# Two graph-attention layers on one core: shorter links between edge pieces, one exponential, a two-piece first product, counts kept, one-hot columns by twos

## The chip, the core and the metric

The kernel runs on 1 core of one Trainium2 chip. A core has a matrix engine (TensorE; PE in the profile, its weight loads PEld), a vector engine (VectorE; DVE), a scalar engine for pointwise functions (ScalarE; ACT), a general engine (GpSimd; POOL), which here issues the gathers, and a sync engine (SyncE; SP), which issues the other transfers. Each engine works through its own instructions in their order; between engines semaphores keep the order. TensorE writes its products to PSUM, which has eight banks.

The metric is the device time of one execution in microseconds: 4405.09 us is the median of 20 runs (4392.43 to 4416.41). The profile page and the trace are of one execution of its own.

## The reference

A graph of 6250 nodes and 200000 edges, sorted by destination, goes through a layer norm with a relu and then through two graph-attention layers, the first with 4 heads of 64, the second with 1 head of 256:

```python
h = jnp.maximum(_layernorm(x, axis=-1), 0.0)
...
te = relu(edge_attr @ We0 + be0) * exp(x @ Wo0 + bo0)[src][:, None]
s2, d2, ea2 = _add_self_loops(src, dst, te, n)
x = relu(_gat(x, s2, d2, ea2, Wg0, as0, ad0, Wge0, ae0, bg0, n, HEADS, PH) + x)
...
def _gat(x, src, dst, ea, Wg, a_s, a_d, Wge, a_e, b, n, h, f):
    hx = (x @ Wg).reshape(n, h, f)
    he = (ea @ Wge).reshape(-1, h, f)
    al = leaky_relu(einsum(hx, a_s)[src] + einsum(hx, a_d)[dst] + einsum(he, a_e), 0.2)
    m = segment_max(al, dst, num_segments=n)
    al = exp(al - m[dst])
    al = al / segment_sum(al, dst, num_segments=n)[dst]
    out = segment_sum(hx[src] * al[:, :, None], dst, num_segments=n)
    return out.reshape(n, h * f) + b
```

A self loop is added to each node, with the mean of its edges' features (their sum divided by their count). So each layer needs, for each destination node, a maximum over its edges, an exponential, and sums of 256 weighted features, of the weights, of the edge features' logits and of the count.

## The kernel before

The 200000 edges are cut into 66 steps (`cuts`): 64 of 24 chunks of 128 edges and two at the end of 14 and 13. Both layers run the same 66 steps, 132 in all, laid out by hand in `edges` (L555 to L653); the last step of a layer is `last` (L655). A prologue computes the node table of layer 0 (`T[0]`: each node's 256 features, its logit parts, its layer-norm numbers).

In a step, 128 partitions hold the step's edges in order, partition p the edges 24p to 24p+23. In the order of the program, for step k (`st`), with nx the step after, pv the one before, pf the one before that:

- SP loads: for every pair of steps the one-hot row numbers `lb` of the pair that comes next (`load_lb`, when k is even; 384 KB), the table rows `tw` of nx's nodes (`nodes`, L834) and in layer 0 their input rows (L836), the edge features `ea` of a pair (`load_ea`, 768 KB, one buffer), the flags `fl` (`load_fl`, every second step, one buffer), and the index tables of a group of four steps. At the step's end SP stores the row of the next layer's table (`rows3`, L1203).
- POOL: 24 gathers (L775) of one table row for each of 128 edges, into one of three buffers `G`. A buffer is free when the sums of the step three before are done.
- `rphase1(nx)`: the first product of the edge features (L853) in four pieces, each into one of two PSUM buffers of one bank (`y`), evicted with a relu by ScalarE (L854).
- `logits(st)`: VectorE adds the parts of the attention logits and runs two scans (L951, L953), a forward and a backward running maximum within each partition.
- `ends(st)`: two TensorE transposes of the scans' ends (L964, L965), which ScalarE brings to SBUF as `LF` (L967).
- `spread(nx)`: VectorE turns nx's row numbers into one-hot columns in place (L870, 128x768) and makes the selection matrix `Q` (L872). Then `parts(nx)` (L892 to L895) splits the destination logits of `tw` into three bf16 parts, and TensorE multiplies them with Q (L897).
- `sums(pv)`: 24 products of one-hot matrices and `G` (L1068), accumulated in one bank.
- `links(st)`: over the 128 partitions, one scan each way (L984, L985) joins the maxima of destinations that run over several partitions, with the flags of which partitions belong together added (L981), and starts from the step before (L979); two small transposes (L990) bring them back. They stand behind `sums(pv)` on TensorE.
- `blocks(nx)`, `onehots(st)` (L882: 24 one-hot matrices by one comparison), `finish(pf)`: the merging of the sums with the self loop (`merge`, then `nodes0` or `nodes1`). `merge` computes from the count column a reciprocal and a mark for nodes without edges (L1091 to L1094).
- `evict(pv)`, `carry(pv)`, `rows1(pf)`: ScalarE and TensorE work on the sums; `rphase2(nx)`, `adst(nx)`: further products for nx's logits.
- `maxima(st)`: VectorE takes the maximum of both scans and both links (L1000 to L1010, the first link waits for L990), subtracts it (L1012), ScalarE computes the exponential twice, once into PSUM for the scaling (L1014) and once into `G` for the sums (L1015); for the edges that continue from the step before there is a third small one (L1025 to L1029).
- `scale(st)`: `G` times the weights, in pieces of 12 chunks (L1058). `carried(st)`: the carried sum is added to the first edge's row. `edge_rows(nx)`: the logits of nx's edges are turned (L925) for the next step.

Between the layers `added` (L739) adds to the first step's gathered rows, chunk by chunk, the rows of the last 256 nodes, which were not in the table yet when they were gathered: for each of 24 chunks two products into a `y` buffer (L745) and an addition by VectorE (L748).

Of the kernel before, what the change touches and what calls it, by code (L numbers as in the profile page):

```python
# [22 lines left out]
F32 = mybir.dt.float32  # L23
BF = mybir.dt.bfloat16
# [7 lines left out]
P = 128  # L32
# [46 lines left out]
class Kernel:  # L79
# [27 lines left out]
    def consts(self, wp):  # L107
# [45 lines left out]
        self.k_iota, self.k_part, self.k_w = k[:, 0:P], k[:, P:P + 1], k[:, 2 * P:2 * P + 4 * C]  # L153
# [205 lines left out]
    def fixed_rows(self):  # L359
        nc, cp = self.nc, self.cp  # L360
        self.crow = cp.tile([1, D + self.L[0].H], F32, name="crow")
        self.cl = [cp.tile([4, 2, P], F32, name=f"cl{i}") for i in range(2)]
        for t in self.cl:
            nc.gpsimd.memset(t[:, 1, P - 1:P], -BIG)
# [20 lines left out]
    def indices(self, wp):  # L385
# [11 lines left out]
        r4 = wp.tile([NS, 4, P], I32, name="r4", bufs=1)  # L397
        nc.sync.dma_start(r4, a["prow"])
        nc.sync.dma_start(self.src, a["src"])
        yield  # L400
        scf = wp.tile([P, 11, NS], F32, name="scf", bufs=1)
# [28 lines left out]
        fl = wp.tile([NS, 3, P], F32, name="fl", bufs=1)  # L430
        wh = wp.tile([NS, 2, P], F32, name="wh", bufs=1)
        V.tensor_tensor(fl[:, 0, :], r4[:, 0, :], r4[:, 3, :], op=OP.is_equal)
        V.tensor_tensor(wh[:, 0, :], r4[:, 2, :], r4[:, 3, :], op=OP.is_equal)
        yield
        V.tensor_tensor(wh[:, 1, :], r4[:, 0, :], r4[:, 1, :], op=OP.is_equal)
        V.tensor_tensor(fl[:, 1:3, :], wh, fl[:, 0:1, :].to_broadcast([NS, 2, P]), op=OP.mult)
        yield
        V.tensor_scalar(fl, fl, 1.0, BIG, op0=OP.subtract, op1=OP.mult)
        self.flags = self.dp.tile([NS, 3, P], F32, name="flags")
        nc.sync.dma_start(self.flags, fl)  # L440
# [61 lines left out]
    def index_group(self, g, pool, di):  # L502
# [22 lines left out]
        for pen, e in ((self.fpen, 0), (self.lpen, c - 1)):  # L525
            t = pool.tile([P, 4 * C], F32, name="gt", bufs=2)
            ends = d3[:, :, e:e + 1].to_broadcast([P, n, c])
            V.tensor_sub(v3(t[:, :w]), *((ends, d3) if e else (d3, ends)))
            yield
            V.tensor_scalar(pen[:, o:o + w], t[:, :w], 1.0, -BIG, op0=OP.min, op1=OP.mult)  # L530
            yield
# [23 lines left out]
    def edges(self, ctx):  # L555
# [7 lines left out]
        self.ps_y = self.pool("ps_y", 2, ctx, space=PSUM)  # L563
        self.ps_1 = self.pool("ps_1", 1, ctx, space=PSUM)
        self.ps_f = self.pool("ps_f", 1, ctx, space=PSUM)
        offs = np.concatenate([[0], np.cumsum(self.cs)]).tolist()
# [144 lines left out]
    def redirect(self):  # L711
# [6 lines left out]
        lt = self.wp.tile([P, 4 * C], F32, name="mt")[:, :c]  # L718
# [20 lines left out]
    def added(self, st, rows):  # L739

        nc, L, c = self.nc, st["L"], st["C"]
        for i in range(self.early):
            ps = self.ps_y.tile([P, 512], F32, name="y")
# [42 lines left out]
    def load(self, k, name, tile, part):  # L786
# [3 lines left out]
        for i, st in enumerate(q):  # L790
            st[name] = tile[:, i]
# [25 lines left out]
    def load_fl(self, k):  # L817
        if self.pair(k):
            H = self.steps[k]["L"].H
            self.load(k, "fl", self.lp.tile([4, 2, 3, P], F32, name="fl", bufs=1), lambda s, e, st: (  # L820
                lambda t: t[:H], self.flags[s:e].partition_broadcast(H)))
# [22 lines left out]
    def rphase1(self, st):  # L844
        nc, L = self.nc, st["L"]
        l, ea = L.l, st["ea"]
        st["R"] = R = self.wp.tile([P, 2, 32 * C], F32, name="R", bufs=1)
        for i in range(2):
            r = slice(i * PH, (i + 1) * PH)
            for w, _ in self.halves(st):  # L850
                n = w.stop - w.start
                y = self.ps_y.tile([P, 512], F32, name="y")
                nc.tensor.matmul(y[:, :n], self.webd[l][r, :], ea[r, w], start=True, stop=True)  # L853
                nc.scalar.activation(R[:, i, w], y[:, :n], AF.Relu, bias=self.be[l])  # L854
                yield
# [9 lines left out]
    def spread(self, st):  # L865


        lb, n = st["lb"], 32 * st["C"]
        V = self.nc.vector
        V.tensor_tensor(lb[:, :n], lb[:, :n], self.k_part.to_broadcast([P, n]), op=OP.is_equal)  # L870
        st["Q"] = Q = self.wp.tile([P, P], BF, name="Q")
        V.tensor_tensor(Q.rearrange("p (k j) -> p k j", j=32), self.k_iota[:, 0:32].unsqueeze(1).to_broadcast([P, 4, 32]),  # L872
# [555 lines left out]
```

## Time and profile before

| | |
|---|---|
| median of 20 runs | 4405.09 us (4392.43 to 4416.41) |
| the profiled execution | 4419.34 us, of which its span 4417.6 us |
| PE busy | 2853.4 us (65%), granted clock 0.768 |
| VectorE busy | 2932.0 us (66%), 7162 instructions |
| ScalarE busy | 688.0 us (16%) |
| POOL busy | 2977.4 us (67%), of which 3114 gathers 2960.9 |
| moved by DMA | 584.83 MB, 132 GB/s over the span |

The span is the time from the first to the last instruction that the profile shows. A group or a timeline row names the line, the engine, the operation, what it writes and reads, the shapes, and in brackets how long its engine had been idle before it and what ended that idling. "issue" is idle time in which the engine waited for nothing that the profile shows. Layer 0 takes the first half of the span (to about 2385 us), layer 1 the second.

### The profile page before, as it was taken

The numbers are of one execution on the slowest core, as the hardware profiler recorded it, in microseconds if no ns is written. First come the engines' busy times: TensorE is split into PE (matmuls) and PEld (weight loads), VectorE is DVE, ScalarE is ACT, GpSimd is POOL, SyncE is SP. The second block draws the span as 40 slices with busy tenths as digits, with TensorE's granted clock in tenths as the row PEclk, the third lists the DMA queues.
The fourth block names the chain that finished last, engine by engine and source line by source line (L and its number), as shares of the span: only waits on it lengthen the run. The fifth ranks groups of instructions, "written<-read, shape, count | busy, mean of one in ns | idle before, by whom it ended". The sixth has DMA issues, their size and how long they took to land. (4 is left out here: it accounts for less than half of the span.)

```text
span 4417.6 us, 37687 instructions
## 1 busy us (share of the span) xinstructions
PE 2853.4 (65%) x10408; PEld 1869.3 (42%) x10408; DVE 2932.0 (66%) x7162; ACT 688.0 (16%) x1910; POOL 2977.4 (67%) x3155
## 2 busy tenths in 40 slices
PE   6756666666666666666665766666666666666665
PEld 5434333343434334343433544434434434434434
DVE  7766676676767667666776666666666666666665
ACT  5111111111111111111111111111111111111110
POOL 2766666666666666666663777777777777777774
PEclk9777777777777777777777878778778778778777
DMA  7554444545444454544442455555555555455552
GB/s 221 144 131 120 128 129 128 132 119 134 118 131 129 129 134 115 134 117 128 126 132 82 133 141 143 142 140 136 135 142 143 142 139 136 135 141 143 142 134 68
DMA packets 246387, 584.83 MB, mean 132 GB/s; under 512 B 62904, under 2 KB 103310, under 8 KB 246104
## 3 DMA queue, kind: packets, MB, share of 16 engines
q0 software_dynamic: 150144, 422.82, 37.4%
q1 hardware_dynamic: 95610, 158.89, 11.6%
q8 instruction: 83, 1.36, 0.1%
q14 instruction: 134, 1.10, 0.1%
q10 hardware_dynamic: 416, 0.67, 0.0%
HBM read 547.87 MB, written 34.37 MB: 132 GB/s over the span
## 5 line engine op out<-in xcount | busy, mean ns | idle before, releaser
L775 POOL DMA_INDIRECT G<-T,src x3114 | 2960.9, 951 | 1382.7 <-issue 902.5
L1068 PE MATMUL u<-G,S 128*128 128x270 f32 (+1 forms) x6252 | 1735.1, 445 | 7.0 <-issue 4.9
L1068 PEld LDWEIGHTS u<-G,S 128*128 128x128 f32 x6252 | 1384.0, 224 | 310.4 <-issue 5.5
L1058 DVE TENSOR_TENSOR G<-G,kps 128x3072 f32<-128x3072 f32 (+1 forms) x270 | 862.9, 3238 | 61.9 <-ACT kps L1014 61.7
L853 PE MATMUL y<-ea,webd 64*128 64x384 f32 (+1 forms) x1056 | 500.3, 604 | 381.2 <-ACT R L854 375.1
L853 PEld LDWEIGHTS y<-ea,webd 64*128 64x128 f32 x1056 | 210.1, 222 | 600.1 <-ACT R L854 481.2
L882 DVE TENSOR_TENSOR S<-kps,loc 128x3072 f32<-128x3072 f32 (+2 forms) x133 | 434.7, 3268 | 0.2 <-ACT kps L1014 0.2
L964 PE MATMUL lf<-ident,bw 128*4 128x128 f32 (+1 forms) x132 | 48.8, 370 | 594.6 <-DVE bw L953 594.6
L854 ACT ACTIVATE R<-y,webd 128x384 f32<-128x384 f32 (+2 forms) x528 | 295.4, 572 | 373.7 <-PE y L853 358.1
L897 PE MATMUL zad<-a,Q 128*128 128x12 bf16 (+1 forms) x132 | 24.9, 189 | 461.1 <-DVE LF L979 427.1
L964 PEld LDWEIGHTS lf<-ident,bw 128*4 128x4 f32 (+1 forms) x132 | 10.7, 81 | 706.0 <-DVE bw L953 685.6
L1004 DVE SCALAR_TENSOR_TENSOR m<-fpen,lf,m 128x24 f32<-128x24 bf16 (+1 forms) x66 | 16.6, 251 | 350.1 <-PE lf L990 350.1
L892 DVE CAST a<-tw 128x4 bf16<-128x4 f32 (+1 forms) x132 | 22.6, 171 | 319.1 <-DMA tw<-T 319.0
L897 PEld LDWEIGHTS <-Q 128*128 128x128 bf16 x132 | 13.7, 104 | 512.3 <-DVE LF L979 490.7
L862 PE MATMUL zad<-R,wea 128*64 128x384 f32 (+1 forms) x1056 | 201.6, 504 | 0.3 <-DVE aq L904 0.3
L939 DVE TENSOR_TENSOR G<-rt,G 128x96 f32<-128x96 f32 (+1 forms) x132 | 30.2, 229 | 247.3 <-DMA G<-T,src 242.2
L1007 DVE TENSOR_TENSOR mt<-fpen,lf 128x96 f32<-128x96 bf16 (+1 forms) x66 | 16.6, 252 | 262.6 <-PE lf L990 262.6
L1073 ACT ACTIVATE U<-u 128x270 f32<-128x270 f32 (+1 forms) x132 | 51.8, 393 | 773.0 <-PE u L1068 773.0
L967 ACT ACTIVATE LF<-lf 4x256 f32<-4x256 f32 (+1 forms) x132 | 49.4, 374 | 595.4 <-PE lf L965 595.3
L925 DVE STREAM_TRANSPOSE rt<-zad 128x768 f32<-128x768 f32 (+1 forms) x130 | 124.4, 957 | 11.5 <-PE zad L911 11.5
L870 DVE TENSOR_TENSOR lb<-lb,kps 128x768 bf16<-128x768 bf16 x132 | 121.1, 918 | 12.1 <-DMA lb<-locrow 12.1
L1117 ACT ACTIVATE mw<-mw 128x8 f32<-128x8 f32 x66 | 13.8, 208 | 717.7 <-DVE mw L1116 717.7
(206 smaller groups left out, 2641.4 us busy)
## 6 DMA issues: line engine op xcount, KB each, us to landing
G<-T,src POOLq DMA_INDIRECT x3114, 2.8
ea<-in_ea_dram SPq DMA_DIRECT2D x64, 768.0 KB
lb<-locrow SPq DMA_DIRECT2D x64, 384.0 KB
T<-t1row SPq DMA_DIRECT2D x66, 260.0 KB
tw<-T SPq DMA_DIRECT2D x66, 258.0 KB
tw<-T SPq DMA_DIRECT2D x66, 134.0 KB
tw<-in_x_dram SPq DMA_DIRECT2D x66, 128.0 KB
out_dram<-fb SPq DMA_DIRECT2D x64, 128.0 KB
```

Of the source, the lines that this page charges most:

```text
L775: nc.gpsimd.indirect_dma_start(out=G[:, c, 0:L.TW], out_offset=None, in_=self.rows[L.l][0:n * (1 + L.l), :], in_offset=bass.IndirectOffset ...
L853: nc.tensor.matmul(y[:, :n], self.webd[l][r, :], ea[r, w], start=True, stop=True)
L854: nc.scalar.activation(R[:, i, w], y[:, :n], AF.Relu, bias=self.be[l])
L862: nc.tensor.matmul(st["zad"][i * PH:(i + 1) * PH, o], self.wea[l][0], R[:, i, w], start=True, stop=False)
L870: V.tensor_tensor(lb[:, :n], lb[:, :n], self.k_part.to_broadcast([P, n]), op=OP.is_equal)
L882: nc.vector.tensor_tensor(st["S"][:, c0:c1, :], self.k_iota.unsqueeze(1).to_broadcast(w), self.loc[:, o + c0:o + c1].unsqueeze(2).to_broad ...
L925: V.transpose(rv[:, :32 * c].rearrange("p (b n) -> p b n", b=2), z.rearrange("p (b n) -> p b n", b=2)[:, :, :16 * c])
L964: nc.tensor.transpose(pl[0:H, P + 1:2 * P + 1], bv[:, :, 0], self.ident)
L967: nc.scalar.activation(lf[:H, 1:2 * P + 1], pl[0:H, 1:2 * P + 1], AF.Copy)
L1058: nc.vector.tensor_tensor(v, v, pw[:, c0:c1, :].unsqueeze(3) .to_broadcast([P, c1 - c0, H, L.F]), op=OP.mult)
L1068: nc.tensor.matmul(u[:, :L.W], S[:, i, :], G[:, i, 0:L.W], start=(j == 0), stop=(j == c - 1))
L1073: self.nc.scalar.activation(U[:, :L.W], st["u"][:, :L.W], AF.Copy)
```

## The change

Line numbers of the kernel after are higher by up to 31. What it does, part by part:

- *Links and ends.* Forward and backward scans now write one tile `fb`, so that the ends of both lie at one stride, those of the backward scan 32 columns on. One transpose of 36 columns (`ends`) brings them to partitions 0 to 3 and 32 to 35 of a PSUM tile `lf` that is kept for the whole run, with its first column at -1e38. The link scans read it there, with no eviction, with no addition of a first flag and with no column from the step before: both flags and the penalties at each piece's first and last edge (`fpen`, `lpen`) now compare with the neighbouring edge across the border. The result is one tile of 36 rows, turned back by one transpose.
- *One exponential.* The carried part's argument is put behind the weights' arguments in the constant tile `mt`, one activation covers all, and VectorE copies the weights to `G`.
- *Scaling* takes 24 chunks in one instruction.
- *First product.* `y` is one buffer of two banks; two products go into it, and one activation evicts both. `added` uses the same single buffer.
- *Counts.* In layer 0 the reciprocal and the mark are written to a tile kept for the run (`cnt`); layer 1 reads them.
- *One-hot columns by twos.* `spread` handles both steps of a pair when it is called for the first, and does nothing for the second.
- *Flags* are loaded for four steps at a time, in two transfers.

```diff
-        self.ps_y = self.pool("ps_y", 2, ctx, space=PSUM)
+        self.ps_y = self.pool("ps_y", 1, ctx, space=PSUM)
...
+        self.lf = self.ps_1.tile([P, 512], F32, name="lf")
+        nc.vector.memset(self.lf[0:4, 0:1], -BIG)
...
-            ps = self.ps_y.tile([P, 512], F32, name="y")
+            ps = self.ps_y.tile([P, 1024], F32, name="y")
...
     def load_fl(self, k):
-        if self.pair(k):
...
+        q = self.steps[k:k + 4]
+        if q and q[0]["s"] % 4 == 0:
+            q = [st for st in q if st["L"] is q[0]["L"]]
+            s, n = q[0]["s"], len(q)
+            fl = self.lp.tile([36, 4, P + 1], F32, name="fl", bufs=1)
+            for i in range(2):
+                to = fl[32 * i:32 * i + 4, :n, :].rearrange("h s p -> h (s p)")
+                self.nc.sync.dma_start(to, self.flags[i, s:s + n].rearrange("s p -> (s p)").partition_broadcast(4))
...
     def rphase1(self, st):
...
-            for w, _ in self.halves(st):
-                n = w.stop - w.start
-                y = self.ps_y.tile([P, 512], F32, name="y")
-                nc.tensor.matmul(y[:, :n], self.webd[l][r, :], ea[r, w], start=True, stop=True)
-                nc.scalar.activation(R[:, i, w], y[:, :n], AF.Relu, bias=self.be[l])
-                yield
+            y = self.ps_y.tile([P, 1024], F32, name="y")
+            for w, o in self.halves(st):
+                nc.tensor.matmul(y[:, o], self.webd[l][r, :], ea[r, w], start=True, stop=True)
...
+                nc.scalar.activation(R[:, i, :32 * c].rearrange("p (b n) -> p b n", b=2),
+                                     y.rearrange("p (b n) -> p b n", b=2)[:, :, :16 * c], AF.Relu, bias=self.be[l])
+            yield
...
     def spread(self, st):
-        lb, n = st["lb"], 32 * st["C"]
+        if "Q" in st:
+            return
         V = self.nc.vector
-        V.tensor_tensor(lb[:, :n], lb[:, :n], self.k_part.to_broadcast([P, n]), op=OP.is_equal)
...
+        q = self.pair(st["k"]) or [st]
+        if len(q) < 2 or q[0]["C"] != q[1]["C"]:
+            q = [st]
+        i, n, s = len(q), 32 * st["C"], st["s"]
+        lb = st["lb2"] if i > 1 else st["lb"].unsqueeze(1)
+        Q = self.wp.tile([P, 2, P], BF, name="Q")
+        V.tensor_tensor(lb[:, :, :n], lb[:, :, :n], self.k_part.unsqueeze(2).to_broadcast([P, i, n]), op=OP.is_equal)
...
     def ends(self, st):
-        nc.tensor.transpose(pl[0:H, P + 1:2 * P + 1], bv[:, :, 0], self.ident)
-        nc.tensor.transpose(pl[0:H, 1:P + 1], fv[:, :, c - 1], self.ident)
-        st["lf"] = lf = self.wp.tile([4, 2 * P + 2], F32, name="LF")
-        nc.scalar.activation(lf[:H, 1:2 * P + 1], pl[0:H, 1:2 * P + 1], AF.Copy)
+        e = st["ends"]
+        self.nc.tensor.transpose(self.lf[0:e.shape[1], 1:P + 1], e, self.ident)
 
     def links(self, st):
...
-            V.tensor_copy(lf[:H, 0:1], prev["lf"][:H, P:P + 1])
-        d1 = self.wp.tile([4, 2, P], F32, name="d1", bufs=1)
-        V.tensor_add(d1[:H], bass_blocks(lf[:H, :], P), fl[:H, 0:1, :].to_broadcast([H, 2, P]))
...
+        V.tensor_tensor_scan(cl[:H, :], fl[:H, :], lf[:H, 0:P + 1], init, op0=OP.add, op1=OP.max)
+        r = slice(32, 32 + H)
+        V.tensor_tensor_scan(cl[r, 0:P - 1][:, ::-1], fl[r, 2:P + 1][:, ::-1], lf[r, 2:P + 1][:, ::-1], -BIG,
+                             op0=OP.add, op1=OP.max)
...
-        for i in (1, 0):
-            nc.tensor.transpose(pc[:, i * H:(i + 1) * H], cl[:H, i, :], self.ident[0:H, 0:H])
+        n = 32 + H
+        st["pc"] = pc = self.lf[:, 160:160 + n]
+        nc.tensor.transpose(pc, cl[:n, 0:P], self.ident[0:n, 0:n])
 
     def maxima(self, st):
...
-        nc.scalar.activation(self.k_w[:, :n], t[:, :n], AF.Exp)
-        nc.scalar.activation(G[:, :c, L.p:L.p + H].rearrange("p c h -> p h c"), th, AF.Exp)
-        yield
+        if st["prev"] is not None:
+            pr = t[0:1, n:n + H]
...
+                V.tensor_sub(pr, pc[0:1, 0:H], mh[0:1, :, 0])
+                yield
+                V.tensor_scalar(pr, pr, -1e4, None, op0=OP.max)
+            yield
+        nc.scalar.activation(self.k_w[:, :n + H], t[:, :n + H], AF.Exp)
         V.tensor_tensor(G[:, :c, L.m:L.m + H].rearrange("p c h -> p h c"), mh,
                         self.isl[:, o:o + c].unsqueeze(1).to_broadcast([P, H, c]), op=OP.mult)
         yield
...
-            nc.scalar.activation(pr[:, :H], pr[:, :H], AF.Exp)
-            yield
+        V.tensor_copy(G[:, :c, L.p:L.p + H].rearrange("p c h -> p h c"),
+                      self.k_w[:, :n].rearrange("p (h c) -> p h c", c=c))
+        yield
+        st["pr"] = self.k_w[0:1, n:n + H]
...
-    def scale(self, st, piece=12):
+    def scale(self, st, piece=C):
...
     def merge(...):
+        if L.l == 0:
+            one = U[:, L.one:L.one + 1]
+            V.tensor_scalar(rc, one, 1.0, None, op0=OP.max)
+            yield
+            V.reciprocal(rc, rc)
+            V.tensor_scalar(nb, one, 0.0, -BIG, op0=OP.is_equal, op1=OP.mult)
+            yield
```

## The prediction

> **What bounds the kernel now.** I read the page first, then one stretch of each layer by busy time and by waits, then the order of time in two neighbouring steps of layer 0 and at the passage between the layers. The page gives no engine more than 67% of the span, so the bound has to be read by stage. These are the two steady stretches, layer 0 and layer 1 (columns: length, busy and count of PE, PEld, DVE, ACT, POOL, then granted clock, DMA share, GB/s):
>
> ```profile
> 200.00:2340.00 2140.00, 1372.65 (x4819) 876.49 (x4819) 1468.75 (x3585) 336.01 (x960) 1382.16 (x1457) 0.75 0.48 126
> 2560.00:4330.00 1770.00, 1146.89 (x4304) 761.67 (x4303) 1127.08 (x2524) 239.82 (x648) 1339.86 (x1413) 0.78 0.52 139
> ```
>
> The last "x" is the number of gathers (L775). In layer 1 one takes 1770/1413 = 1.253 us, in layer 0 2140/1457 = 1.469. A step has 24 of them: 30.1 us a step in layer 1, 35.3 in layer 0. The waits of layer 1 (who waited for whom: us, times, longest):
>
> ```profile
> POOL G L775 <- issue: 421.3, 1383, 0.3
> ...
> DVE G L939 <- DMA G<-T,src: 234.2, 58, 4.9
> ```
>
> and those of VectorE in layer 0:
>
> ```profile
> DVE a L892 <- DMA tw<-T: 298.4, 33, 12.1
> DVE mt L1007 <- PE lf L990: 245.7, 61, 4.8
> ```
>
> In layer 1 POOL has only its 0.30 us between gathers (421.3/1383) and VectorE waits for the gathered rows, 234.2/58 = 4.0 us in each step. Layer 1 is set by POOL, with 4 us of room for everybody else. In layer 0 it is the other way round: POOL waits for a free buffer (327.6 us in 55 steps, by the same view), and VectorE waits for something in every step. Two steps in order of time, an odd one (first three lines) and the even one after it:
>
> ```profile
> 1543.74 0.93 DVE L870 TENSOR_TENSOR lb<-lb,kps 128x768 bf16<-128x768 bf16 x1
> 1544.59 0.28 DVE L872 TENSOR_TENSOR Q<-kps,qsel 128x128 bf16<-128x128 f32 x1
> 1544.79 0.18 DVE L892 CAST a<-tw 128x4 bf16<-128x4 f32 x1
> ...
> 1573.86 0.92 DVE L870 TENSOR_TENSOR lb<-lb,kps 128x768 bf16<-128x768 bf16 x1
> 1574.70 0.28 DVE L872 TENSOR_TENSOR Q<-kps,qsel 128x128 bf16<-128x128 f32 x1
> 1584.19 0.41 DVE L892 CAST a<-tw 128x4 bf16<-128x4 f32 x1 [9.21 <-DMA tw<-T]
> ...
> 1585.32 13.97 PE L1068 MATMUL u<-G,S 128*128 128x270 f32 x48
> ...
> 1601.97 6.62 DVE L1058 TENSOR_TENSOR G<-G,kps 128x3072 f32<-128x3072 f32 x2 [0.57 <-ACT kps L1014]
> ```
>
> From L870 to the next L870 the odd step takes 1573.86 - 1543.74 = 30.1 us; the even one ends at the next L870, 1613.63, and takes 39.8. Both are one chain: VectorE up to `parts` (L892), TensorE's product with Q (L897, at 1585.27), the 24 sums of the step before (L1068, 14 us), the links' transposes behind them (L990; VectorE's L1007 waits for them until 1599.54), maxima, exponential (1601.68), scaling (L1058), back to the next logits. The even step has 9 to 12 us more, because `tw` is asked for behind a pair's one-hot rows on SP's queue:
>
> ```profile
> 1570.35 0.60 SPq L800 DMA_DIRECT2D lb<-locrow  x1
> 1571.95 0.34 SPq L834 DMA_DIRECT2D tw<-T  x1
> 1572.82 0.34 SPq L836 DMA_DIRECT2D tw<-in_x_dram  x1
> 1575.55 0.40 SPq L800 DMA_DIRECT2D ea<-in_ea_dram  x1
> ```
>
> SP gets there only when the table row's store (L1203, 1569.88) is released, and `tw` lands 12.2 us after its issue, whatever VectorE does meanwhile. So in layer 0 a microsecond counts only if it lies (a) between L892 and the table row, in any step, or (b) between the table row and L892 in an odd step. What VectorE does before L892 in an even step, and between L897 and L1007 in any step, is covered.
>
> **The change, part by part.** Layer 0 has 31 odd and 31 even full steps before its last three.
>
> *Links and ends.* Gone are one transpose (L964/L965 become one), the eviction LF (0.37 on ACT), the copy L979 (0.13) and the addition L981 (0.41); the scans stay. All lie between L897 and L1007, under the sums, where VectorE already idles 245.7/61 = 4.0 us; cost without that cover -0.9 us a step, with it 0. Two L990 transposes become one: the pair takes 0.28 us and one alone 0.21 in its row, so -0.07 on the chain in each step (0 to -0.15, since the new one is 36 wide).
>
> *One exponential.* The second one (L1015) and the small one (L1029) go, off the chain. The two small subtractions (0.15 and 0.16) now stand before the exponential; they end 1601.4, and the exponential starts at 1601.68 only because ACT is with h1T until then, so 0 (0.3 if ACT were free). New is a copy of the 96 weights into G on VectorE, after the exponential and before the scaling. Nearest rows: L1017 writes the same places, and the next instruction starts 0.17 us after it; its whole row is 0.32. I take 0.20 (0.17 to 0.36).
>
> *Scaling in one piece.* Two instructions of 128x3072 take 6.62 together, and at 3351 ns each they overlap by 0.08; -0.07.
>
> So each of 62 steps gains 0.20 and loses 0.07 and 0.07: +0.06, **+4 us** (-6 to +19).
>
> *One-hot columns by twos.* `spread` tests both steps of a pair when the even one is next, which is in an odd step, and does nothing in an even step. In the even step the saved 0.85 + 0.20 lie before the wait for `tw`: 0. In the odd step they double in place (b). L870 takes 928 ns for 768 columns and 594 for 448, that is 1.04 ns a column: +0.80 for 768 more; L872 +0.13 for 128 more. 31 x 0.93 = **+29 us**. Its end is late, then L892, L897 and the sums.
>
> *First product in two pieces.* `ps_y` keeps two banks but one buffer. In a step the second pair of products starts after a 768-wide eviction instead of a 384-wide one, 0.4 us later (the row of 384 is 577 ns, 192 is 413: 0.85 ns a column), and ends some 0.4 later. In odd steps ends' transpose has 1.3 us of room there, in even steps it is under the `tw` wait: 0. SP's load of `ea` goes out 0.4 us later in every second even step; behind it is the store L1203, 35 us later: 0.
>
> *The same buffer in `added`*, at the passage. Now:
>
> ```profile
> 2434.23 24.31 PE L745 MATMUL y<-t1row,S 128*128 128x260 f32 x96
> ```
>
> 24 rounds of 1.01 us back to back, VectorE's addition (425 ns) beside the next round. With one buffer product and addition alternate: 23 times the addition 0.43, two handoffs of 0.05 and a bare weight load's exposed part 0.12, 0.65 in all, **+15 us**. Lower bound the addition alone, 23 x 0.425 = 10. Upper bound: the same four-part product after idling took 2.10 us (L379 at 2413.34), so 23 x (1.09 + 0.6) = 39. I take 15, since L745 itself ran at 1.01 from its first rounds on, straight after TensorE's idling. The page "TensorE: Matmul & The Clock Gate" of the Trainium skill (What's actually happening) lets the clock fall to half only after about 3.4 us of idling; pauses of 0.6 us would then leave it, an estimate that makes this part 15 and not 39; no run here shows such pauses yet. "Perfetto Trace Analysis" (Matmuls) speaks against this edit: groups should rotate through banks so that one's evacuation overlaps the next.
>
> *Passage, other parts.* The last step of layer 0 (L655) draws two pieces of the first product before its maxima; these are now all of it, and ACT evicts both before the exponential: two cold products (2.92) and evictions 1.0 and 1.0 against what it did before 2392.34, +2.2, less 0.65 for links: +1.5 (0 to 3). Steps 66 and 67, which have no long waits yet: ends' transpose stands behind the slower first product (+1), `spread` saves 1.1 in 66 and adds 0.93 in 67, links save some: with the copies **+2** (0 to 3). None of the passage is hidden: POOL waits there 6.19 us, until 2493.86, for step 66's sums, and never again, so what is late here is late at the end.
>
> *Counts kept, flags by fours, edge penalties.* Three small VectorE instructions less in each step of layer 1: that layer is POOL's, 0; at the kernel's end links and counts save about 1 us. SP issues two flag loads every fourth step in place of one every second, at the same place of its queue, ahead of a store that waits anyway: 0. The penalties keep their number of instructions. New memsets and a small load in the prologue: +0.5.
>
> Sum: 4 + 29 + 15 + 1.5 + 2 + 0.5 - 1 = **+51 us**. The profiled execution ran 4419.3 (span 4417.6), so 4470; it stood 14.3 over the median of 4405.1, where the same sum gives **4456**. With the bounds (-6 to 19; 10 to 39; 0 to 6; pair tests at 29): +32 to +93, 4437 to 4498.
>
> **Rivals.**
> - *The pair test is absorbed* in the odd step: 4456 - 29 = 4427. For it: VectorE idles 3.7 to 4.8 us there. Against: that idling (L1007) is for sums that cannot start before L897, which the test delays.
> - *Slow product at the passage*: 23 x (2.10 - 1.01) = +25, 4481. For: L379 and L862 ran at that pace just before; against: L745 reached 1.01 at once.
> - *Faster, since `tw` comes sooner.* `tw` shares the DMA queues with `ea` (768 KB), which now goes out later in every second even step. When lb and ea were small (step 62) the wait was 4.9 instead of 9.2: 4.3 us x 16 = -69, giving 4387. It decides from 51/16 = 3.2 us per such step. Against: the delay is 0.4 us, and steps where `ea` follows at once wait only 2 us longer.
> - *The change doesn't do what it says where it counts*: all of it falls under POOL's 30 us; 4405. Against: POOL's waits in layer 0.
>
> **How the numbers follow.** Forecast 0.64, absorbed test 0.11, slow product 0.09, sooner `tw` 0.10, no effect 0.06. A measurement of this kernel can tell about 0.2% (9 us) from no change. Faster 0.10, same 0.07, slower 0.83. The range reaches down over the absorbed test and up over most of the slow product: 4424 to 4490.
>
> **What would show it.** Right: layer 1 still at 30.1 us a step with VectorE waiting for G; in layer 0 odd steps at 31, even ones as before with the wait for `tw` 1 us longer; a test of 1.7 us over 128x1536 in odd steps only; L745's rounds at 1.6 to 1.7 us; POOL's wait near 2500 about 23 us. Wrong: even steps under 38 us, or odd ones unchanged.

## The result and the profile after

The changed kernel takes 4464.61 us (median of 7 runs, 4458.90 to 4473.89), the kernel before, run beside it, 4407.76 (47 runs). The ratio is 1.0133, with a 95% interval of 1.0121 to 1.0145: 57 us slower. The forecast was 4456.

The profiled execution of the changed kernel took 4469.84 us, its span is 4468.1: 50.5 us more than the span before. These two profiles don't stand alike to their medians: the one before is 11.6 us above its 4407.8, this one 5.2 above its 4464.6. Stage by stage (a step is counted from the last instruction that forms its logits on VectorE, ahead of the scans: L945 before, L984 after; the first step is number 0):

| place | before | after | difference |
|---|---|---|---|
| start of the span to the first logits | 123.1 | 136.9 | +13.8 |
| layer 0, first three steps | 81.5 | 81.4 | -0.1 |
| layer 0, the 59 steps after them (3 to 61) | 2075.1 | 2085.7 | +10.6 |
| the next two | 65.7 | 65.1 | -0.6 |
| passage (steps 64 to 67) | 158.5 | 183.1 | +24.6 |
| layer 1 (steps 68 to 128) | 1828.5 | 1830.1 | +1.6 |
| tail (last three steps and the end) | 85.2 | 85.7 | +0.5 |

The two steady stretches of the changed kernel by busy time (columns as before: length, PE, PEld, DVE, ACT, POOL with their counts, granted clock, DMA share, GB/s):

```profile
200.00:2340.00 2140.00, 1338.14 (x4670) 861.64 (x4669) 1440.34 (x3379) 271.99 (x653) 1388.46 (x1459) 0.75 0.48 126
2600.00:4370.00 1770.00, 1132.12 (x4182) 757.23 (x4181) 1089.59 (x2183) 172.79 (x353) 1340.45 (x1411) 0.77 0.52 139
```

Gathers are the measure of progress again. Layer 1 does 1411 in 1770 us, 1.254 us each, as before (1.253): it is still POOL's. Fewer instructions there (2183 on VectorE in place of 2524, 353 on ScalarE in place of 648) change nothing, and VectorE still waits for the gathered rows in each step, 4.2 us of it now, 4.0 before (who waited for what: us, times, longest; 2600 to 4370 us):

```profile
DVE G L978 <- DMA G<-T,src: 249.3, 59, 5.8
```

Layer 0 does 1459 gathers in 2140 us where it did 1457.

An odd step of layer 0 and the even one after it, VectorE in order of time:

```profile
1574.33 1.73 DVE L906 TENSOR_TENSOR lb<-lb,kps 128x1536 bf16<-128x1536 bf16 x1
1575.97 0.42 DVE L907 TENSOR_TENSOR Q<-kps,qsel 128x256 bf16<-128x256 f32 x1
1576.31 0.17 DVE L931 CAST a<-tw 128x4 bf16<-128x4 f32 x1
...
1592.79 0.32 DVE L1055 COPY G<-kps 128x96 f32<-128x96 f32 x1 [0.57 <-ACT kps L1051]
1592.97 6.54 DVE L1086 TENSOR_TENSOR G<-G,kps 128x6144 f32<-128x6144 f32 x1
...
1613.52 0.35 DVE L931 CAST a<-tw 128x4 bf16<-128x4 f32 x1 [8.40 <-DMA tw<-T]
```

The pair test and Q stand in the odd step and last 1.73 and 0.42 us; from L906 to L931 it is 1.98 us, where the kernel before took 1.05 (1543.74 to 1544.79). In the even step there is no L906, and L931 waits for `tw` just the same. Over 200 to 2340 us these waits are 319.1 us, where they were 298.4, so 0.6 us longer in the mean of 33:

```profile
DVE a L931 <- DMA tw<-T: 319.1, 33, 13.1
```

The copy into G delays the scaling by 0.18 us.

The rounds of `added` at the passage, two additions and the product between them:

```profile
2461.60 0.42 DVE L766 TENSOR_TENSOR G<-G,y 128x260 f32<-128x260 f32 x1 [0.45 <-PE y L763]
2462.07 1.08 PEld L763 LDWEIGHTS y<-t1row,S 128*128 128x128 f32 x4 [1.21 <-DVE G L766]
2462.08 1.38 PE L763 MATMUL y<-t1row,S 128*128 128x260 f32 x4 [0.52 <-DVE G L766]
2463.49 0.42 DVE L766 TENSOR_TENSOR G<-G,y 128x260 f32<-128x260 f32 x1 [1.47 <-PE y L763]
```

Product and addition take turns: the weights are loaded 0.05 us after the addition ends, and 1.42 us later the next addition starts. A round is 1.90 us, all 23 of them alike; before it was 1.00. POOL, which waits out the passage, shows the sum of it (columns: busy, mean ns, idle before it and what ended it, 2480 to 2560 us):

```profile
L793 POOL DMA_INDIRECT G<-T,src x42 | 39.7, 945 | 41.2 <-PE lf L1018 28.7 <-issue 12.2 <-DVE a L931 0.3
```

The 28.7 us are the wait that took 6.2 before (the row of the kernel before):

```profile
2493.86 0.94 POOL L775 DMA_INDIRECT G<-T,src  x1 [6.19 <-ACT U L1073]
```

And in the prologue there is a wait that was not there at all (who waited for what: us, times, longest):

```profile
DVE before L410 <- DMA dpv<-in_dpv_dram: 6.8, 1, 6.8
```

VectorE's first test of one-hot rows divides the prologue in two. It starts 10.5 us later than before, and from it to the first logits it takes 16.20 us (120.75 to 136.95), 3.35 more than the 12.85 of before (110.21 to 123.06):

```profile
110.21 0.95 DVE L870 TENSOR_TENSOR lb<-lb,kps 128x768 bf16<-128x768 bf16 x1 [12.09 <-DMA lb<-locrow]
...
120.75 1.75 DVE L906 TENSOR_TENSOR lb<-lb,kps 128x1536 bf16<-128x1536 bf16 x1 [12.69 <-DMA fl<-flags]
```

### The profile page after: what moved, and what is told of

Its sections match the earlier page's. It is cut to its first block, busy times and chain, and to the rows that moved or that the text cites. A ratio compares the mean times of both kernels' runs of the same rounds, so it can differ in the third digit from the quotient of the medians.

```text
span 4468.1 us, 35036 instructions
## 1 busy us (share of the span) xinstructions
PE 2826.5 (63%) x10144; PEld 1864.8 (42%) x10144; DVE 2871.3 (64%) x6578; ACT 545.3 (12%) x1256; POOL 2983.9 (67%) x3158
## 4 chain that ended last, share of the span: by engine, by line
POOL 30%; PE 24%; DVE 19%; issue 12%; DMA 11%; SPq 2%; ACT 1%; DVEq 0%; ACTq 0%; POOLq 0%
POOL G L793 30%; PE u L1096 21%; DVE G L1086 10%; DMA tw<-T 8%; DMA G<-T,src 1%; DVE lb L906 1%; PE fin L1107 1%; PE fin L1191 1%; DVE G L1075 1%; DVE rt L964 1%; ACT carry L1109 1%; DVE G L1055 0%; SPq L818 0%; SPq L849 0%; DVE t1row L389 0%
## 5 line engine op out<-in xcount | busy, mean ns | idle before, releaser
L1096 PE MATMUL u<-G,S 128*128 128x270 f32 (+1 forms) x6252 | 1711.4, 441 | 10.5 <-DVE G L1086 10.5
L1096 PEld LDWEIGHTS u<-G,S 128*128 128x128 f32 x6252 | 1364.7, 221 | 663.3 <-issue 196.5
L1086 DVE TENSOR_TENSOR G<-G,kps 128x6144 f32<-128x6144 f32 (+2 forms) x140 | 853.2, 6099 | 0.0
L1001 PE MATMUL lf<-ident,fb 128*36 128x128 f32 (+1 forms) x132 | 54.0, 409 | 536.5 <-DVE fb L993 303.1
L882 ACT ACTIVATE R<-y,webd 128x768 f32<-128x768 f32 x260 | 232.1, 893 | 607.9 <-PE y L877 596.1
L1001 PEld LDWEIGHTS lf<-ident,fb 128*36 128x36 f32 (+1 forms) x132 | 15.8, 120 | 653.5 <-DVE fb L993 377.6
L931 DVE CAST a<-tw 128x4 bf16<-128x4 f32 (+1 forms) x132 | 21.3, 161 | 333.3 <-DMA tw<-T 333.1
L978 DVE TENSOR_TENSOR G<-rt,G 128x96 f32<-128x96 f32 (+1 forms) x132 | 30.1, 228 | 261.0 <-DMA G<-T,src 255.5
L1134 ACT ACTIVATE mw<-mw,mg 128x2 f32<-128x2 f32 x66 | 19.7, 298 | 880.1 <-DVE mg L1133 880.1
L906 DVE TENSOR_TENSOR lb<-lb,kps 128x1536 bf16<-128x1536 bf16 (+1 forms) x68 | 112.9, 1661 | 12.7 <-DMA fl<-flags 12.7
L891 PEld LDWEIGHTS zad<-R,wea 128*64 128x64 f32 x1056 | 65.5, 138 | 96.9 <-issue 58.8
L1107 PE MATMUL fin<-U,lsel 128*1 128x270 f32 (+1 forms) x260 | 79.1, 385 | 40.5 <-ACT U L1101 21.5
```

The lines of the kernel that those rows point to most:

```text
L882: nc.scalar.activation(R[:, i, :32 * c].rearrange("p (b n) -> p b n", b=2), y.rearrange("p (b n) -> p b n", b=2)[:, :, :16 * c], AF.Relu, ...
L891: nc.tensor.matmul(st["zad"][i * PH:(i + 1) * PH, o], self.wea[l][0], R[:, i, w], start=True, stop=False)
L906: V.tensor_tensor(lb[:, :, :n], lb[:, :, :n], self.k_part.unsqueeze(2).to_broadcast([P, i, n]), op=OP.is_equal)
L1001: self.nc.tensor.transpose(self.lf[0:e.shape[1], 1:P + 1], e, self.ident)
L1086: nc.vector.tensor_tensor(v, v, pw[:, c0:c1, :].unsqueeze(3) .to_broadcast([P, c1 - c0, H, L.F]), op=OP.mult)
L1096: nc.tensor.matmul(u[:, :L.W], S[:, i, :], G[:, i, 0:L.W], start=(j == 0), stop=(j == c - 1))
```

## The experiments

All are compared with the kernel before on the same chip. Chips differ; ratios are carried from one to another, and numbers by place come from the profiles, one of each kernel.

### First four runs, on a chip that takes 15% longer

`a_spread1`: `spread` as it was before, the rest changed.

```
-        if "Q" in st:
-            return
+        lb, n = st["lb"], 32 * st["C"]
         V = self.nc.vector
...
-        V.tensor_tensor(lb[:, :, :n], lb[:, :, :n], self.k_part.unsqueeze(2).to_broadcast([P, i, n]), op=OP.is_equal)
...
+        V.tensor_tensor(lb[:, :n], lb[:, :n], self.k_part.to_broadcast([P, n]), op=OP.is_equal)
```

> The changed kernel, with the pair test taken back: each step tests its own one-hot columns again (128x768, 0.93 us, and Q over 128 columns). Theory (the forecast's step): the second test stands in the odd step between the table row and TensorE's product with Q, so odd steps go from 30.43 to 29.5 us, 31 x -0.93 = -29 us, even steps stay; 4436 us. Rival 1: the sums give back part of it (they ran 0.38 us faster in the odd steps of the changed kernel): odd steps to 29.8, -19 us, 4445. Rival 2: it is absorbed, odd steps stay at 30.4, 0 us. Rival 3: the gain of every second even step (39.41 to 38.47) came from the same edit and goes with it: +14 us back, 4450 in all.

`a_dpv`: the copy of L410 moved to the end of `indices`.

```
         yield
-        self.before = cp.tile([P, NS], F32, name="before")
-        V.tensor_copy(self.before, dpv)
         scf = wp.tile([P, 11, NS], F32, name="scf", bufs=1)
...
         self.direct = max(NS - 2, 0)
         yield
+        self.before = cp.tile([P, NS], F32, name="before")
+        V.tensor_copy(self.before, dpv)
```

> The changed kernel, with the copy of the small dpv load (L410) moved from the start of the index work to its end, where its load has long landed. Theory: VectorE, in order, stood 6.8 us at the copy in the prologue, and all behind it was late; the first logits come 7 to 8 us earlier (136.9 to about 129), nothing else moves; 4457 us. Rival: what follows waits for the other loads behind it anyway, 0 us, 4464.

`a_added2`: halves of one two-bank tile in turn.

```
+        y = self.ps_y.tile([P, 1024], F32, name="y")
         for i in range(self.early):
-            ps = self.ps_y.tile([P, 1024], F32, name="y")
+            ps = y[:, 512 * (i % 2):512 * (i % 2) + 512]
```

> The changed kernel, with `added` using the two banks of one tile in turn (round i in half i mod 2), nothing else. Theory: the single buffer makes the round 1.90 us in place of 1.01; it goes back to 1.0 and the 24 rounds from 45.5 us to 24.3; POOL's wait at the passage shrinks with it; -21 us, 4443. Rival 1: something else set the round (a cold product, as elsewhere at the passage): 1.7 us or more, -5 us or less. Rival 2: the rounds shorten but the passage waits for something else, half of it is lost: -10 us.

`a_undo4`: the three together, and in `last` one `next(y, None)` ahead of the maxima in place of two.

> The changed kernel with four things taken back at once: the pair test, the early dpv copy, the single bank in `added`, and one of the two pieces of the next step's first product that `last` draws before its maxima. Theory: the four add up, -29 -8 -21 -2.5 = -60 us, 4404, the time of the kernel before. Rival 1: the pair test gives only 5 to 19 us, 4414 to 4428. Rival 2: what is left of the change (the links with one transpose, one exponential, counts kept, the first product in two pieces) is itself a gain of 10 us or more: 4390 or less.

The kernel before took 5064.23 us here, 15% more than on the other chips. The ratios to it are 0.9946 [0.9931, 0.9960], 0.9946 [0.9926, 0.9966], 0.9950 [0.9932, 0.9968] and 0.9920 [0.9906, 0.9934]. So every variant of the changed kernel is half a per cent or more *faster* here than the kernel before. The third run stands for the changed kernel itself, since its edit shortened nothing: its first rounds in `added` are 1.90 us as in the changed kernel. The two halves belong to one buffer, and the product still waited for the addition on the other half. (The fourth has the same edit there.)

What this chip does is seen in `a_added2` at the end of a group of sums of layer 1 and, in a second stretch, in its `added` (TensorE in order of time):

```profile
3205.66 12.88 PE L1097 MATMUL u<-G,S 128*128 128x261 f32 x45
3219.74 0.38 PE L1097 MATMUL u<-G,S 128*128 128x261 f32 x1 [1.21 <-issue]
3222.55 0.59 PE L1097 MATMUL u<-G,S 128*128 128x261 f32 x1 [2.42 <-issue]
3224.64 0.59 PE L1097 MATMUL u<-G,S 128*128 128x261 f32 x1 [1.50 <-issue]
...
2707.73 2.14 PE L764 MATMUL y<-t1row,S 128*128 128x260 f32 x4 [8.36 <-issue]
2718.93 2.14 PE L764 MATMUL y<-t1row,S 128*128 128x260 f32 x4 [9.06 <-issue]
```

After 12.9 us of matmuls in a row the last three stand idle for 1.2 to 2.4 us each with nothing that the profile shows to wait for; in `added` the rounds grow to 11.2 us, at a granted clock of 0.50 from 2690 to 2740 us. Layer 1 takes 2128.6 us in place of 1830, and POOL, which in the changed kernel's profile waits for nothing longer than 0.3 us there, waits for a product of TensorE in almost each step (2900 to 4900 us of `a_added2`):

```profile
POOL G L794 <- PE lf L1019: 280.8, 56, 6.0
```

So TensorE, not POOL, paces this chip, and none of the four runs bears on the terms of the forecast. Why the change wins half a per cent here stays open: there is no profile of the kernel before on this chip.

### One part at a time, on the usual chips

`a_undo5`: as `a_undo4`, with two real banks in `added`:

```
-            ps = self.ps_y.tile([P, 1024], F32, name="y")
+            ps = (self.ps_f.tile([P, 512], F32, name="fin") if i % 2 else
+                  self.ps_y.tile([P, 1024], F32, name="y"))
```

> The changed kernel with four things taken back, `added` now truly with two banks: its odd rounds go into the bank of `fin`, which is idle there. Theory, by place: first logits 7 to 8 us sooner (the dpv copy), odd steps of layer 0 from 30.43 to 29.5 us (the pair test, -29), rounds of `added` from 1.90 to 1.01 us (-21), the step before it 2.5 us shorter; in all -60, 4404 us where the changed kernel takes 4464.6. Rival 1: the pair test gives only 5 to 19 us because sums or even steps give it back: 4414 to 4428. Rival 2: the remaining edits are a gain of their own: 4390 or less. On a chip whose TensorE is throttled harder (the last four runs: the kernel before at 5064, matmuls standing 1.5 to 2.5 us at the end of each group of sums), only the rounds' length and the first logits are to be read against these numbers.

`b_spread2`: the kernel before with the new `spread` (and `load`'s second name for the pair's tile), nothing else.

> The kernel before, with the one-hot columns by twos alone. Theory (the forecast's step): odd steps of layer 0 from 29.81 to 30.7 us, even ones unchanged (41.9 and 39.4), +29 us, 4437. Rival 1: the shift of 0.9 us makes the sums run faster or `tw` land sooner, odd +0.6 and every second even step -0.9, as in the changed kernel: +5 to +10, 4415. Rival 2: absorbed, 0.

`b_y1`: the kernel before with the new `rphase1`, the new `added` and `ps_y` with one buffer.

> The kernel before, with the first product evicted in two pieces through one two-bank buffer, in the loop and in `added`, and nothing else. Theory: rounds of `added` 1.01 to 1.90 us, +21; `last` +2; first logits +2 to +3; every second even step either as before (39.4; +25 in all, 4432) or, if the later issue of `ea` is what let `tw` land sooner, 38.5 (-14; +11 in all, 4418). Rival: the slower first product reaches the chain in odd steps (TensorE's queue ahead of ends' transpose), +0.4 a step: 4444.

`b_twfirst`: the kernel before with one line moved (in the last step of a layer it stands where it stood, ahead of `last`).

```
-            self.load_lb(k + 2)
...
             if st["s"] + 1 == self.NS:
+                self.load_lb(k + 2)
                 self.last(st, pv, nx)
...
             self.gather(nx)
             self.nodes(nx)
+            self.load_lb(k + 2)
             drain(self.rphase1(nx))
```

> The kernel before, with one thing moved: in each step SP issues the loads of the next step's node rows (`tw`, x) ahead of the pair's one-hot rows (`lb`), not behind them. Theory: the 9 to 12 us of an even step are the queue behind 384 KB; they go, even steps come to 30 to 32 us, 31 x -9.3 = -288 us, about 4120. Rival 1: then POOL's gathers or the DMA engines bind layer 0, steps at 33 to 35 us: -120 to -200 us. Rival 2: `tw` is late because of the store of the table row and `ea`, not of `lb`: 0.

`a_dpv_b`: the same kernel as `a_dpv`.

> The changed kernel with the dpv copy moved to the end of the index work, on a chip of the usual kind if it is one (the kernel before near 4400 us); the first try of it fell on the slow chip. Theory: first logits from 136.9 to about 129 us, nothing else moves: -8 us, 4457 where the changed kernel takes 4464.6. Rival: what follows the copy waits for the loads behind it anyway: first logits stay at 137, 4465.

`a_fin`: the changed kernel with `added` as in `a_undo5`, nothing else.

> The changed kernel with two banks in `added` (odd rounds in the bank of `fin`) and nothing else. Theory: rounds from 1.90 to 1.00 us, all 21 us come off the passage and the total: 4444. Rival: with the rounds shortened the passage waits for the gathers or for the index work, and only half of it comes off: 4454.

Times by place (us; "even 4" are the even steps that are multiples of four, "even 2" the others; steps 3 to 61 of layer 0; a round is the mean of the 23 in `added`):

| kernel | ratio to before, 95% | first logits | odd | even 4 | even 2 | sums in odd, clock in them | round | passage |
|---|---|---|---|---|---|---|---|---|
| before | 1 | 123.1 | 29.81 | 41.93 | 39.41 | 13.49, 0.828 | 1.00 | 158.5 |
| changed | 1.0133 [1.0121, 1.0145] | 136.9 | 30.43 | 42.27 | 38.47 | 13.11, 0.851 | 1.90 | 183.1 |
| a_undo5 | 1.0011 [0.9998, 1.0025] | 126.8 | 30.01 | 41.45 | 37.74 | 13.44, 0.830 | 1.00 | 157.2 |
| b_spread2 | 1.0053 [1.0037, 1.0069] | 124.9 | 30.44 | 42.00 | 38.45 | 13.25, 0.843 | 1.00 | 159.2 |
| b_y1 | 1.0071 [1.0057, 1.0086] | 128.2 | 29.84 | 41.38 | 38.71 | 13.52, 0.826 | 1.90 | 183.0 |
| a_dpv_b | 1.0129 [1.0110, 1.0148] | 131.6 | 30.49 | 41.38 | 38.30 | 13.23, 0.844 | 1.90 | 180.6 |
| a_fin | 1.0098 [1.0080, 1.0116] | 135.6 | 30.41 | 42.01 | 37.79 | 13.12, 0.851 | 1.00 | 159.9 |
| b_twfirst | 0.9426 [0.9412, 0.9441] | 125.2 | 30.06 | 32.64 | 30.08 | 13.72, 0.813 | 1.00 | 151.5 |
| a_twfirst | 0.9535 [0.9520, 0.9551] | 138.6 | 30.35 | 32.28 | 30.17 | 13.10, 0.852 | 1.90 | 176.2 |
| a_undo5_tw | 0.9458 [0.9444, 0.9473] | 130.3 | 30.03 | 32.42 | 30.40 | 13.38, 0.833 | 1.00 | 152.9 |

What follows:

- *The pair test.* Alone it costs 0.53%, 23 us (16 to 30), and odd steps go from 29.81 to 30.44. Absorbed it is not. But it isn't 0.93 us a step either: from the logits to L931 the odd step is 0.90 us longer in `b_spread2` and 0.96 in the changed kernel, and the sums that follow are 0.24 and 0.38 us shorter. The reason is in the clock. Two groups of sums in odd steps, one of each kernel, each as a whole and then in its two parts, first before, then changed (columns as in the table of stretches):

```profile
1545.69:1559.01 13.32, 13.32 (x50) 10.52 (x51) 9.04 (x25) 1.12 (x3) 9.98 (x11) 0.84 0.43 114
1545.69:1550.02 4.33, 4.33 (x11) 3.31 (x12) 4.25 (x5) 0.00 (x0) 3.37 (x4) 0.50 0.49 128
1550.02:1559.01 8.99, 8.99 (x41) 7.21 (x40) 4.79 (x21) 1.12 (x3) 6.61 (x7) 1.00 0.40 107
```

```profile
1577.16:1590.12 12.96, 12.96 (x50) 10.28 (x49) 8.56 (x24) 1.12 (x3) 8.52 (x10) 0.86 0.40 108
1577.16:1580.75 3.59, 3.59 (x9) 2.79 (x9) 3.54 (x4) 0.00 (x0) 2.68 (x4) 0.50 0.41 105
1580.75:1590.12 9.37, 9.37 (x42) 7.50 (x41) 5.02 (x21) 1.12 (x3) 5.85 (x7) 1.00 0.40 109
```

  Length times granted clock is 11.19 and 11.15: the same work. The granted clock is not 0.84 or 0.86 but 0.50 at first and then 1.00, and so it is in each of the 59 groups of steps 3 to 61 in every kernel of the table. What differs is how long a group stays at 0.50: in odd steps 4.68 us in the mean before, 4.18 in `b_spread2`, 3.92 in the changed kernel, and half of that time is lost. In every kernel of the table with the pair test the mean clock of these groups is 0.843 to 0.852, in every one without it 0.813 to 0.833. A quarter to two fifths of the delay comes back in this way. That the longer pause ahead of the group is the reason does not hold: even steps pause some 10 us longer, and their groups stay at 0.50 for 4.88 us before and 4.85 in the changed kernel. In each profile all changes of the clock lie whole multiples of 3.41 us apart. If the change comes at an instant of such a grid, a group that starts later has less time at 0.50 ahead of it and wins back up to half of its delay; that would fit, but no run tests it by itself.

- *The single bank in `added`.* `b_y1` alone costs 31 us (25 to 38), of which the rounds are 23 x 0.90 = 20.6; `a_fin` takes the rounds back, the passage falls from 183.1 to 159.9, and the ratio from 1.0133 to 1.0098 (two chips; -15 us, with some 10 to either side). Nothing else at the passage takes the place of the wait. The rest of `b_y1` is in the profile at the first logits (128.2, where the three kernels with the old prologue in this respect have 123.1 to 125.2: +3 to +5) and in step 66 (17.3 to 20.6 us, +3.3; 18.5 in the changed kernel), where the transposes of the scans' ends come right behind the second pair of the first product.

- *The copy of L410.* In `a_dpv_b` the wait is gone and the first logits come at 131.6 us; in the three kernels with the early copy (changed, `a_fin`, `a_twfirst`) at 135.6 to 138.6, 137.0 in the mean: -5.4, not -8. In the total this can't be told from nothing (1.0129 against 1.0133). The first test of one-hot rows shows where the time goes:

| kernel | the test starts | from it to the first logits |
|---|---|---|
| before, `b_twfirst` | 110.2, 112.3 | 12.85, 12.86 |
| `b_spread2` (pair test) | 110.6 | 14.28 |
| `b_y1` (first product in two pieces) | 113.1 | 15.06 |
| `a_undo5`, `a_undo5_tw` (first product, no early copy) | 111.5, 114.0 | 15.26, 16.23 |
| `a_dpv_b` (both, no early copy) | 114.7 | 16.93 |
| changed, `a_fin`, `a_twfirst` (all) | 120.8, 119.8, 121.7 | 16.20, 15.80, 16.93 |

  The early copy puts the test back by 6 to 7 us. Behind it the pair test costs 1.4 us and the first product through one buffer 2.2. Kernels that are alike in this differ by 2 to 3 us in the start of the test and by up to 1.1 in what follows.

- *`tw`.* The even steps of all kernels that keep its order lie at 41.4 to 42.3 and 37.7 to 39.4 us; the longest of the second kind, by 0.7 us, are those of the profile before. `b_spread2` and `b_y1`, of which only the second issues `ea` later, have the same 38.5 and 38.7 in the "even 2" steps: the later `ea` is not what shortens them.

- *What is left.* `a_undo5` keeps the links, the scaling in one piece, the one exponential, the counts, the flags by fours and the two pieces in the loop, and stands at 1.0011, -1 to +11 us.

The run `b_twfirst` is the test of the reading that all else rests on. The even steps lose 9.3 us, odd ones gain 0.25, the total falls by 5.7% to 4143.52 us. SP's queue and VectorE around two steps of it:

```profile
1063.13 0.35 SPq L1204 DMA_DIRECT2D T<-t1row  x1
1064.02 0.34 SPq L835 DMA_DIRECT2D tw<-T  x1
...
1066.59 0.93 DVE L871 TENSOR_TENSOR lb<-lb,kps 128x768 bf16<-128x768 bf16 x1
1067.64 0.17 DVE L893 CAST a<-tw 128x4 bf16<-128x4 f32 x1
...
1094.38 0.44 SPq L499 DMA_DIRECT2D gi<-in_dnx_dram  x1
1095.43 0.34 SPq L835 DMA_DIRECT2D tw<-T  x1
1095.96 0.34 SPq L837 DMA_DIRECT2D tw<-in_x_dram  x1
1096.33 0.93 DVE L871 TENSOR_TENSOR lb<-lb,kps 128x768 bf16<-128x768 bf16 x1
1096.40 0.60 SPq L801 DMA_DIRECT2D lb<-locrow  x1
...
1098.55 0.18 DVE L893 CAST a<-tw 128x4 bf16<-128x4 f32 x1 [1.09 <-DMA tw<-T]
```

Issued right behind the store of the table row, `tw` (the cast at 1067.64) is there in time; from issue to use it has 3.6 us, and behind `lb` it took 12.2. In the fourth steps two index loads (L499) still go ahead of it, and 1.09 us of wait are left. Layer 0 then does a gather every 1.278 us (1447 in 1850 us), 1.469 before: it is almost POOL's too.

### The change on the new order

`a_twfirst` and `a_undo5_tw` are the changed kernel and `a_undo5` with the same line moved.

> The changed kernel with the next step's node rows asked for ahead of the pair's one-hot rows. Theory: even steps lose their stall as the kernel before did (41.9 and 39.4 to 32.6 and 30.1 us), about -250 us; the second pair test in odd steps then costs 0.6 to 0.9 us but the even steps, no longer under a stall, save up to 0.9 each: layer 0 as in the reordered kernel before, while the 14 us of the prologue and the 24 of the passage stay: 4143 + 38 = about 4181. Rival 1: odd steps pay and even ones gain nothing, because `tw` still ends last in them: +20 more, 4200. Rival 2: POOL binds all of layer 0, steps at 30.1 us and no trace of the pair test: 4170.

> The kernel with the four edits taken back (pair test, early dpv copy, single bank in `added`, two pieces in `last`) and node rows ahead of one-hot rows: what is left of the change are the links, the one exponential, the counts and the first product in two pieces. Theory: +0.11 us a step from the copy into G, the other terms under cover: 62 x 0.11 = +7 us and +4 in the prologue against the reordered kernel before, -2 at the end: 4152. Rival: with layer 0 no longer stalled the shorter links show, -0.9 us a step: 4143 - 56 = 4087.

They take 4187.76 and 4154.58 us (0.9535 and 0.9458). Against the reordered kernel before (0.9426) that is, by the ratios, +48 and +14 us. In `a_twfirst` the odd steps pay 0.29 us, the even ones gain 0.36 or lose 0.09, so layer 0 comes out 4.7 us longer in the 59 steps (1812.5 to 1817.2); the prologue (+13.4) and the passage (+24.7) stay in full. Shorter links show no gain even now: `a_undo5_tw` is at 4154.6 where the rival had 4087. (With steps of 30.7 us in the mean and POOL's 30.1 there was no more than 0.6 us a step to gain.) The best kernel of all that ran is the kernel before with the one line moved, `b_twfirst`: 0.9426 of the kernel before.

## Why the prediction was right, point by point

- *What bounds.* Layer 1 is POOL's: +1.6 us for all that was taken out of it. At the end, where the forecast had -1, it is +0.5. Layer 0's even steps are set by `tw` behind `lb`: shown by `b_twfirst`.
- *Links, exponential, scaling: +4.* By place, in the steps shown: the copy +0.18, the scaling -0.08, the transposes -0.03, the maxima with the two subtractions ahead +0.04; +0.11 x 62 = 7. In the mean of 30 odd steps, from the end of the sums to the next logits, it is 13.55 against 13.50 us: 3. The forecast's lower bound of -6 does not come out of its own numbers: (0.17 - 0.15 - 0.07) x 62 is -3. That the removed LF, addition and transpose gain nothing that a run can tell is seen twice, in `a_undo5` and, with the `tw` stall away, in `a_undo5_tw`.
- *One-hot columns by twos: +29.* Right in place and mechanism, mis-sized: the delay is 0.96 (0.93 forecast), but the sums behind it spend less time at half the clock and give 0.24 to 0.38 back, so it is +0.62 a step, 19 us by the odd steps and 23 (16 to 30) by `b_spread2`. The forecast took the length of the sums as fixed.
- *First product in two pieces: 0 in the loop.* Odd steps 29.84 against 29.81 in `b_y1`: right there. Not in step 66 (+3.3), nor at the start (+2.2), where the chain runs through it.
- *`added`: +15.* Measured +20.6. The working took two handoffs of 0.05 us and 0.12 for the exposed part of the weight load. The profile has 1.42 us from the weight load of a four-part product that stands alone to the next addition, against 1.01 for one that follows another. So the round is 0.05 + 1.42 + 0.43 = 1.90 us: beside addition and product it has 0.46 us, not 0.22. The choice between the ends was right: TensorE's granted clock in these 43.6 us is 1.00, so the pauses of 0.52 us did not cost it. That is what the rule of the Trainium skill's page "TensorE: Matmul & The Clock Gate" (What's actually happening), that the clock falls after about 3.4 us of idling, says of such pauses. On the slow chip, where pauses of 8.4 and 9.1 us stand between the products, the granted clock was 0.50. One reason for the choice was misread: L745 did not come straight after idling but behind 3.2 us of other products, at a clock of 0.50 until 2434.07, 0.16 us ahead of it; in the changed kernel the clock rises during the first product, which takes 1.91 us. The skill's page "Perfetto Trace Analysis" (Matmuls), which has groups rotate through banks, was right against this edit: two banks in two buffers bring the round back to 1.00.
- *Passage, other parts: +3.5.* Steps 64 to 67 without the rounds: 24.6 - 20.6 = +4.0.
- *Prologue: +0.5.* This step failed, by 13 us. It counted the new instructions and not their waits. VectorE's instructions behind the copy, the normalisation of the nodes among them, stand until it has waited 6.8 us for a fresh load; the first test comes 6 to 7 us sooner where the copy is moved. Two edits that the forecast had costed in the loop only add to it: the first pair test 1.4 us and the first product through one buffer 2.2, on the chain to the first logits. The rest, 3 to 4 us, stays open; like kernels differ by 2 to 3 us in the start of that test alone.
- *The sum.* +51 forecast, +57 measured: prologue 13 short, `added` 6 short, pair test 6 to 10 over. That the whole came this close is partly luck, since these misses offset each other. The parts as measured (13.8, 3 to 7, 19, 20.6, 4.0, 1.6 and 0.5) come to 62 to 67, more than the whole. The two profiles alone show only +10.6 for layer 0's 59 steps where the terms above would have 22 to 25; the profile before had long even steps (0.7 us x 14 for the second kind alone; its run was 11.6 us over the median), so part of that is probably its own scatter. Of the rivals, the slow product (4481) falls with the clock of 1.00; the absorbed pair test (4427) and no effect (4405) fall with `b_spread2`; the sooner `tw` (4387) needed 3.2 us per second even step, and `b_y1` shows less than one, which `b_spread2` shows as well.
- *What would show it.* Odd steps at 30.4, not 31; even ones as before (42.3 and 38.5 against 41.9 and 39.4), with the wait for `tw` 0.6 us longer, not 1; the test 1.73 us over 128x1536; rounds 1.90, above the 1.6 to 1.7; POOL's wait 28.7, not 23.

## What to carry to other kernels

Ask of a moved or merged piece of work whether it lands in the step with slack or in the one without: the pair test saves an instruction in each even step, where VectorE waits anyway, and pays for it in each odd one. A buffer taken from a loop costs in every other loop that shares its pool, and the price counts one product alone (1.42 us here), not the one it has in a row (1.01). A queue is an order: moving one 384 KB load behind two smaller ones that are needed at once gained more than four times what the whole change lost. And a forecast that reaches the sum may still have missed its parts: here the prologue's 13 us were in part made up for by a pair test that cost 6 to 10 less than forecast.

## What the hardware showed that was not expected

- A mean granted clock of 0.8 was here never a clock of 0.8. Each group of 48 matmuls in steps 3 to 61, of every kernel in the table, starts at 0.50 and goes to 1.00 once, 2.8 to 6.2 us later; it takes 11.15 us plus half of the time at 0.50, from 12.6 to 14.2 us. So a group that is delayed by 0.9 us can end only 0.6 later.
- One chip ran the same kernel 15% slower. In a variant of the changed kernel TensorE paused there for 1.2 to 9.1 us where no wait explains it, and against the kernel before this variant had the other sign: 0.995 in place of 1.013. A forecast of one per cent holds for the kind of chip that its profile came from.
